# Seven products of quarters in the feed-forward of an AdaLN block, with factors summed by accumulating transfers

## The chip, the cores and the metric

One Trainium2 chip; the kernel runs on 1 of its cores. The metric is the device time of one execution in microseconds (us), smaller is better. Engines: PE multiplies matrices, DVE (VectorE), ACT (ScalarE) and POOL (GpSimd) do elementwise work, SP issues transfers; each engine works through its own queue of instructions in order. DVE and ACT read PE's results from PSUM banks; POOL works on SBUF only. Transfers (DMA) are issued from SP's, ACT's or POOL's queue.

## The reference

All data are float32: x is [4, 1024, 512], c [4, 512], eight factors of [512, 512].

```python
mod = (_silu(c) @ wmod).reshape(4, 6, 1, -1)
sa, ca, ga, sb, cb, gb = (mod[:, 0], mod[:, 1], mod[:, 2], mod[:, 3], mod[:, 4], mod[:, 5])
ga = (2 * (ga >= 0) - 1) * jnp.maximum(jnp.abs(ga), 0.25)       # gb likewise
h = _layernorm(x) * (1 + ca) + sa
# attention: q = h @ Wq.T and k = h @ Wk.T have 64 columns, shared by all 16 heads
x = x + ga * (merge(softmax(q @ k.T) @ split(h @ Wv.T)) @ Wo.T)
h = _layernorm(x) * (1 + cb) + sb
x = x + gb * (einsum('btd,rde->bte', h, factors) / sqrt(8) + bias)
```

Since the scores are the same for all heads, the value and output weights multiply into one 512x512 matrix (`wvo`), and since the feed-forward is a sum over the eight factors, they add into one 512x512 matrix (`fsum`).

## The kernel before

A batch is 1024 tokens: 8 tiles of 128 tokens (`NT`), two groups of 4 tiles (`GT`). All of the order is written by hand: a `Plan` collects calls with a beat (a number), sorts them by beat and emits them so; calls with the same beat keep the order in which they were entered. `pe(n, ...)` puts PE work at the present beat and moves it on by n beats; `at(beat, ...)` puts other work beside it. Each engine then runs its instructions in the order of emission, waiting by semaphores that the framework derives from the tiles.

Per batch there are these stages:

- `project`: q and k of each group (L393 to L421). Then `plan_scores_and_y`: eight rounds of a y tile (h times the scaled `wvo`, four matmuls of 512 columns, L483) and a tile of scores (L430). For each score tile DVE finds the maximum (L443) and ACT the exponents (L444); each pair of tiles is then transposed by DVE in 32x32 blocks (`turn_probs`, L450) and rearranged by 16 SP transfers of 64 KB (`move_probs`, L325 to L335). `sum_y` makes sums of quarters of y, on DVE for batch 0 and on POOL for the others (L488 to L499).
- `plan_f` of the batch before: `f_tile` (L542) multiplies each tile of h by the scaled factor sum `fb`, four matmuls of 512 columns into one PSUM bank, and DVE adds the bank to x (L549). A finished tile is stored and, where there is a batch after next, a tile of x is loaded in its place, both by POOL's queue.
- `plan_o`: probabilities times y, for pairs of tiles, in seven products of quarters instead of eight (Strassen's way, in Winograd's form). `sum_probs` (L464) makes sums of quarters of the probabilities on DVE. The seven products of a pair (L517 to L538) accumulate in three PSUM banks (y, q, x); after each product DVE adds the bank to the quarter of x where it belongs (L534), while the bank keeps its contents for the next product. A later product into the same bank therefore waits for this addition.

Layer norms are planned beside the attention products: `plan_ln1` for the next batch's first norm, `plan_ln2` for this batch's second. Both take statistics on DVE (L293), the power on POOL (`rstd`, L300), normalise (L309; ACT needs `center`'s product first, DVE does not), transpose on DVE (`turn_h`), move by 16 SP transfers (`move_h`) and apply scale and shift on ACT (`shift_h`, L354). `add_bias` (L555) adds the gated bias to x on POOL.

The last batch has no scores to hide behind: there the plan runs the feed-forward's first group of batch 2, the attention products of batch 3, then the second group of batch 2 and both groups of batch 3 (L709 to L722).

At the start (`plan_start`, L566) the weights, x and the six blocks of `wmod` are loaded, `wvo` is multiplied (L174) and copied out by ACT (L180), the modulation rows are made (L193 to L246), the first layer norm is transposed on PE (L380, `first_out` L389) and the factors are loaded in halves by POOL's queue and added by POOL (`load_factor`, `add_factor`, L251 to L269). Tiles share buffers by tag: "s" has two buffers (sums of probabilities), "yt" and "qT"/"kT" one, PSUM has two banks "y", two double banks "sc", and one each of "q" and "x".

## Time and profile before

| what | time |
|---|---|
| median of 3 runs | 536.98 us (536.24 to 539.12) |
| the profiled execution | 538.23 us |
| its span in the profile | 536.4 us |
| first attention product of batch 0 starts | 88.37 us |
| attention products of batch 1, 2, 3 start | 216.6, 336.7, 443.1 us |
| attention products of batch 3 end | 491.4 us |
| matmuls of `f_tile` (256 records) | 110.5 us busy, 0.592 us mean |
| DVE additions of `f_tile` (32) | 0.685 us mean |
| POOL additions of factors (14) | 2.39 us mean, 33.4 us |
| mean granted PE clock | 0.986 |

A record's duration on PE includes the pipeline; the pace of PE is read from the start of one stage to the start of the next. Durations of DVE, ACT and POOL are those of one instruction from start to end, and the next instruction can start a little before the end. The profile puts an engine's idle time down to what released it. A matmul of this program appears as two records.

### The profile page before, as it was taken

What the parts mean: (1) busy time and instruction counts of PE and PEld (TensorE: products, weight loads), DVE (VectorE), ACT (ScalarE), POOL (GpSimd) and SP (SyncE); (2) the same over time, 40 slices, a digit from 0 to 9 for tenths busy, and PEclk for the clock granted to TensorE, in tenths of its full rate; (3) what the DMA queues carried; (4) which work ended last, traced back from release to release, by engine and by line L of the source; (5) the groups of instructions that cost most, each with busy time, mean ns of one, the idle gap of its engine ahead of it and who ended that gap; (6) DMA issues with size and microseconds to landing.
All of it is one profiled execution on the core that took longest, in us unless ns stands there. A gap on an engine that the chain in (4) does not pass through costs nothing.

```text
span 536.4 us, 5575 instructions
## 1 busy us (share of the span) xinstructions
PE 520.4 (97%) x1738; PEld 306.6 (57%) x1738; DVE 347.6 (65%) x568; ACT 131.5 (25%) x206; POOL 198.0 (37%) x170
## 2 busy tenths in 40 slices
PE   8988998799999999999999999999999999999997
PEld 4343334688743344888743344888743348887442
DVE  3448699899765546689665545789665673784611
ACT  1133322212255410222155310232155310001020
POOL 1038487563144162243145072244144060450600
PEclk9997999799999999999999999999999999999999
DMA  9993589864537679523536679423536677005352
GB/s 321 381 388 116 146 156 216 139 132 106 77 51 106 93 138 227 166 69 79 78 50 104 98 148 226 155 64 80 78 50 110 96 130 139 6 5 76 102 134 78
DMA packets 223342, 68.60 MB, mean 128 GB/s; under 512 B 206528, under 2 KB 207040, under 8 KB 223312
## 3 DMA queue, kind: packets, MB, share of 16 engines
q1 hardware_dynamic: 216704, 48.30, 46.9%
q0 software_dynamic: 5504, 18.88, 10.9%
q10 hardware_dynamic: 1104, 1.06, 0.6%
q8 instruction: 14, 0.23, 0.2%
q14 instruction: 16, 0.13, 0.1%
HBM read 28.33 MB, written 8.41 MB: 68 GB/s over the span
## 4 chain that ended last, share of the span: by engine, by line
PE 88%; DVE 4%; SPq 2%; DMA 2%; ACT 2%; issue 1%; ACTq 0%; DVEq 0%
PE ps_o_y L526 21%; PE ps_f L545 20%; PE ps_y L483 17%; PE ps_o_q L526 10%; PE ps_sc L430 6%; PE ps_o_x L526 5%; PE ps_qk L403 5%; PE ps_wvo L174 3%; SPq L335 2%; PE ps_mod L193 1%; DMA wos<-in_woT_dram 1%; DMA pt<-pr 1%; DVE s L472 1%; DVE pr L453 1%; ACT hT L387 1%
## 5 line engine op out<-in xcount | busy, mean ns | idle before, releaser
L483 PE MATMUL ps_y<-w,hT 128*128 128x512 f32 x256 | 119.2, 609 | 0.0
L545 PE MATMUL ps_f<-f,hT 128*128 128x512 f32 x256 | 110.5, 592 | 0.0
L483 PEld LDWEIGHTS ps_y<-w,hT 128*128 128x128 f32 x256 | 46.8, 192 | 69.2 <-issue 67.6
L545 PEld LDWEIGHTS ps_f<-f,hT 128*128 128x128 f32 x256 | 48.6, 190 | 60.8 <-issue 59.6
L300 POOL TENSOR_TENSOR r<-v,mhalf 128x4 f32<-128x4 f32 x16 | 18.0, 1126 | 148.0 <-DVE v L298 130.9
L354 ACT ACTIVATE hT<-hT,chan,chan 128x512 f32<-128x512 f32 x56 | 41.0, 805 | 116.1 <-DMA hT<-st 116.1
L526 PE MATMUL ps_o_y<-y,pt 128*128 128x256 f32 x256 | 58.5, 379 | 0.0
L549 DVE TENSOR_TENSOR x<-ps_f,x 128x512 f32<-128x512 f32 x32 | 21.9, 685 | 50.7 <-PE ps_f L545 50.7
L526 PEld LDWEIGHTS ps_o_y<-y,pt 128*128 128x128 f32 x256 | 48.6, 190 | 8.3 <-issue 1.9
L293 DVE BATCH_NORM_STATS2 bn<-x 128x6 f32<-128x512 f32 x64 | 43.3, 677 | 6.7 <-DMA x<-in_x_dram 6.7
L555 POOL TENSOR_TENSOR x<-x,bc_gbias 128x512 f32<-128x512 f32 x32 | 43.9, 1394 | 6.1 <-DVE st L319 5.4
L317 ACT ACTIVATE st<-x,m,r 128x512 f32<-128x512 f32 x24 | 17.6, 803 | 112.1 <-DVE m L305 72.5
L443 DVE TENSOR_REDUCE nm<-ps_sc 128x1 f32<-128x1024 f32 x32 | 38.3, 1206 | 5.6 <-PE ps_sc L430 5.6
L534 DVE SCALAR_TENSOR_TENSOR x<-ps_o_y,ri,x 128x256 f32<-128x256 f32 x64 | 30.2, 471 | 17.6 <-PE ps_o_y L526 17.4
L281 POOL TENSOR_TENSOR f<-fsum,bc_gb 128x512 f32<-128x512 f32 x16 | 20.7, 1324 | 54.7 <-DMA bc_gb<-rows_gb 54.7
L444 ACT ACTIVATE pr<-ps_sc,nm 128x1024 f32<-128x1024 f32 x32 | 35.7, 1117 | 19.9 <-DVE nm L443 15.6
L339 DVE STREAM_TRANSPOSE st<-st 128x512 f32<-128x512 f32 x56 | 37.0, 689 | 5.5 <-ACT st L317 5.2
L430 PE MATMUL ps_sc<-kT,qT 64*128 64x512 f32 x128 | 38.8, 663 | 0.0
L453 DVE STREAM_TRANSPOSE pr<-pr 128x2048 f32<-128x2048 f32 x16 | 36.9, 2306 | 2.6 <-DMA pt<-pr 1.7
L269 POOL TENSOR_TENSOR fsum<-fsum,factors 128x1024 f32<-128x1024 f32 x14 | 33.4, 2388 | 11.7 <-DMA factors<-in_factors_dram 11.6
L526 PE MATMUL ps_o_y<-yt,s 128*128 128x256 f32 x128 | 32.1, 396 | 5.0 <-DVE x L534 5.0
L451 DVE RECIPROCAL ri<-den 128x2 f32<-128x2 f32 x16 | 2.6, 165 | 52.5 <-ACT pr L444 52.5
(81 smaller groups left out, 633.2 us busy)
## 6 DMA issues: line engine op xcount, KB each, us to landing
pt<-pr SPq DMA_DIRECT2D x256, 64.0 KB, 2.3
hT<-st SPq DMA_DIRECT2D x224, 64.0 KB, 2.2
factors<-in_factors_dram POOLq DMA_DIRECT2D x14, 512.0 KB, 5.1
wm<-in_wmod_dram SPq DMA_DIRECT2D x6, 1024.0 KB, 9.7
out_dram<-x POOLq DMA_DIRECT2D x24, 256.0 KB, 3.5
x<-in_x_dram SPq DMA_DIRECT2D x16, 256.0 KB, 8.9
x<-in_x_dram POOLq DMA_DIRECT2D x16, 256.0 KB, 4.6
out_dram<-x SPq DMA_DIRECT2D x8, 256.0 KB, 2.0
```

The lines of the kernel that those rows point to most:

```text
L269: nc.gpsimd.tensor_tensor(fsum[:, k, :], fsum[:, k, :], fac[n], ALU.add)
L293: nc.vector.bn_stats(s, xt[b, t])
L339: nc.vector.transpose(s, s)
L354: eng.activation(v, v, AF.Identity, bias=shift, scale=scale)
L430: nc.tensor.matmul(ps_sc[b, i][:, ts(h, 512)], qT[h * R : (h + 1) * R, ts(i, P)], kT[h * R : (h + 1) * R, :], start=True, stop=True,)
L443: nc.vector.tensor_reduce(nm, ps_sc[b, i], AX.X, ALU.max, negate=True)
L444: nc.scalar.activation(probs[b, p][:, :, k].rearrange("p c j e -> p j c e"), ps_sc[b, i].rearrange("p (j c e) -> p j c e", j=NT, c=NQ), AF ...
L453: nc.vector.transpose(v, v)
L483: nc.tensor.matmul(ps, h_rows(1, b, t, kc), wb[b][:, kc, :], start=(kc == 0), stop=(kc == KC - 1))
L526: nc.tensor.matmul(ps, a[:, ts(j, P)], bb[:, j, :], start=(tag is not None and j == 0), stop=(j == GT - 1), skip_group_check=tag is None,)
L545: nc.tensor.matmul(ps, h_rows(2, b, t, kc), fb[b][:, kc, :], start=(kc == 0), stop=(kc == KC - 1))
L555: nc.gpsimd.tensor_tensor(xt[b, t], xt[b, t], bcs["gbias", b], ALU.add)
```

## The change

Every feed-forward group but the last of batch 3 is computed in seven products of quarters: a pair of tiles (two tiles of a group, two apart), the two halves of the 512 features and the two halves of the output columns are the quarters. `product` is the former `o_product` made general; `sum_h` makes the sums of h for a group, `sum_f` those of the factors for a batch. The sums of h take a buffer "s", those of the factors the buffer that q and k of the next batch had (now one tile "qk"), in batch 3 the "yt" buffer; some sums are written over a quarter that is no longer needed. They are on DVE for batches 0 to 2 and on POOL for batch 3. In `plan_f` each product takes 2 beats.

The factors are loaded whole, 1 MB each, into `fsum`, the first by a plain transfer, the other seven by transfers that add; POOL's additions go.

The second layer norm is normalised by ACT instead of DVE for group 0 of every batch and both groups of the last; the additions of the bias are planned 8 to 72 beats later; sums of probabilities, transposes and their moves get other beats, `turn_probs` comes in four pieces, and `move_blocks` goes by columns first.

At the start x and cT are loaded from ACT's queue and the output weights from SP's, batch 0's projections use the banks "sc", the last four modulation rows a bank "y", and the copies of `wvo` come later.

```diff
--- before.py
+++ after.py
@@ -130,14 +130,13 @@
     def load_weights(cc):
         nc.sync.dma_start(out=wvs[:, cc, :], in_=wv[ts(cc, P), :])
-        nc.scalar.dma_start(out=wos[:, cc, :], in_=woT[ts(cc, P), :])
+        nc.sync.dma_start(out=wos[:, cc, :], in_=woT[ts(cc, P), :])
     for cc in range(KC - 1):
         load_weights(cc)
-        load_x(0, cc)
-        if cc == 0:
-            nc.scalar.dma_start(out=cTs, in_=cT.rearrange("(kc p) b -> p kc b", p=P))
-    load_x(0, KC - 1)
+        load_x(0, cc, nc.scalar)
+    load_x(0, KC - 1, nc.scalar)
+    nc.scalar.dma_start(out=cTs, in_=cT.rearrange("(kc p) b -> p kc b", p=P))
     load_wmod(0)
     load_wmod(1)
@@ -175,9 +174,9 @@
...
+    def wvo_out(kc):
+        nc.scalar.copy(wvo[:, kc, :], pw[kc // 2][:, ts(kc % 2, 512)])
     row_tiles = [sp.tile([B, 3, D], F32, tag="s", name=f"rows_{h}") for h in range(2)]
@@ -186,8 +185,8 @@
...
-    def mod_products(ms):
-        ps = psum_mm(f"ps_mod_{ms[0]}", "q")
+    def mod_products(ms, tag):
+        ps = psum_mm(f"ps_mod_{ms[0]}", tag)
@@ -246,27 +245,15 @@
-    def load_factor(n):
...
+    def sum_factor(r):
         if r == 0:
+            nc.gpsimd.tensor_copy(fsum[0:1, 0, 0:1], chans[1][0:1, 0, 0:1])
         nc.gpsimd.dma_start(
+            out=fsum, in_=factors[r].rearrange("(kc p) e -> p kc e", p=P),
+            accum_op=ALU.bypass if r == 0 else ALU.add,
+        )
@@ -330,8 +317,8 @@
             dst = dst.rearrange("p (r w) -> p r w", r=NQ)
-        for r in range(NQ):
-            for c in range(NQ):
+        for c in range(NQ):
+            for r in range(NQ):
@@ -394,11 +381,9 @@
         if g == 0:
-            qkT[b] = (
-                qkp.tile([2 * R, T], F32, tag="qT", name=f"qT_{b}"),
-                qkp.tile([2 * R, T // 2], F32, tag="kT", name=f"kT_{b}"),
-            )
-        ps = psum_mm(f"ps_qk_{b}_{g}")
+            qk = qkp.tile([2 * R, 3 * T // 2], F32, tag="qk", name=f"qk_{b}")
+            qkT[b] = qk[:, :T], qk[:, T:]
+        ps = psum_mm(f"ps_qk_{b}_{g}") if b else psum("sc", T, f"ps_qk_{b}_{g}")[:, :512]
@@ -447,9 +432,10 @@
-    def turn_probs(b, p):
-        nc.vector.reciprocal(rinv[b][:, 2 * p : 2 * p + 2], den[b, p])
-        v = probs[b, p].rearrange("p c k j e -> p (c k j e)")
+    def turn_probs(b, p, c):
+        if c == 0:
+            nc.vector.reciprocal(rinv[b][:, 2 * p : 2 * p + 2], den[b, p])
+        v = probs[b, p][:, c].rearrange("p k j e -> p (k j e)")
@@ -500,53 +486,113 @@
...
+    PLACE = {1: (0, 0), 5: (1, 1), 6: (0, 1), 2: (0, 0), 7: (1, 1), 3: (0, 1), 4: (1, 0)}
+    BANK = {1: "y", 6: "y", 7: "y", 4: "y", 5: "q", 3: "q", 2: "x"}
+    SUMS = {5: 0, 6: 1, 3: 2}
+    TERMS = {5: 0, 6: 1, 4: 2}
+    LEFT = {1: (0, 0), 2: (0, 1), 4: (1, 1), 7: (1, 0)}
+    RIGHT = {1: (0, 0), 2: (1, 0), 3: (1, 1), 7: (0, 1)}
+    ps_p = {}
+    def product(key, n, lefts, rights, add):
+        first = n in (1, 5, 2)
+        if first:
+            ps_p[key, BANK[n]] = psum(BANK[n], H, f"ps_{'_'.join(map(str, key))}_{BANK[n]}")
+        ps = ps_p[key, BANK[n]]
+        for j, (left, right) in enumerate(zip(lefts, rights)):
+            nc.tensor.matmul(
+                ps, left, right, start=(first and j == 0), stop=(j == len(lefts) - 1),
+                skip_group_check=not first,
+            )
+        add(ps, *PLACE[n])
+    def o_product(b, p, n):
+        a = S[b, p][:, SUMS[n]] if n in SUMS else quarter(b, p, *LEFT[n])
+        if n in TERMS:
+            y = YT[b][:, TERMS[n]]
...
+    SF, TF = {}, {}
+    KH = KC // 2
+    def f_left(b, g, ih, kh):
+        v = hT[2, b, g].rearrange("p (k t w) -> p k t w", k=KC, t=GT)
+        return v[:, ts(kh, KH), ts(ih, GT // 2), :].rearrange("p k t w -> p k (t w)")
+    def f_right(b, kh, e):
+        return fb[b][:, ts(kh, KH), ts(e, H)]
+    def sum_h(b, g, n, eng):
+        if n == 0:
...
+        u = SF[b, g]
+        a11, a12, a21, a22 = [f_left(b, g, i, k) for i in range(2) for k in range(2)]
+        o, i0, i1 = [
+            (u[:, 0], a21, a22), (u[:, 1], u[:, 0], a11), (a21, a11, a21), (u[:, 2], a12, u[:, 1])
+        ][n]
+        eng.tensor_tensor(o, i0, i1, ALU.add if n == 0 else ALU.subtract)
+    def sum_f(b, n, eng):
+        if n == 0:
+            pool, tag = (qkp, "qk") if b + 1 < B else (yp, "yt")
...
+        u = TF[b]
+        b11, b12, b21, b22 = [f_right(b, k, e) for k in range(2) for e in range(2)]
+        o, i0, i1 = [
+            (u[:, 0], b12, b11), (u[:, 1], b22, u[:, 0]),
+            (b12 if b + 1 < B else u[:, 3], b22, b12), (u[:, 2], b21, u[:, 1]),
+        ][n]
+        eng.tensor_tensor(o, i0, i1, ALU.subtract)
+    def f_product(b, g, m, n):
+        a = SF[b, g][:, SUMS[n]] if n in SUMS else f_left(b, g, *LEFT[n])
+        f = TF[b][:, TERMS[n]] if n in TERMS else f_right(b, *RIGHT[n])
+        if n == 7 and b + 1 == B:
+            f = TF[b][:, 3]
+        def add(ps, k, e):
+            xi = xt[b, f_pair(g, m)[k]][:, ts(e, H)]
+            nc.vector.tensor_tensor(xi, ps, xi, ALU.add)
+        product(
+            ("f", b, g, m), n,
+            [a[:, k, ts(m, P)] for k in range(KH)], [f[:, k, :] for k in range(KH)], add,
+        )
+    def f_pair(g, m):
+        return g * GT + m, g * GT + GT // 2 + m
@@ -560,8 +606,9 @@
         if k:
-            at(plan.now + 7, turn_probs, b, p)
-            at(plan.now + 8, move_probs, b, p)
+            for c in range(NQ):
+                at(plan.now + 7 + 1.6 * c if p + 1 < NP else plan.now + 12 + 3 * c, turn_probs, b, p, c)
+            at(plan.now + (12 if p + 1 < NP else 22), move_probs, b, p)
     def plan_start():
@@ -574,10 +621,12 @@
             pe(8, wvo_chunk, cc)
-        pe(8, mod_products, [0, 1])
+        pe(8, mod_products, [0, 1], "q")
         at(plan.now, mod_row, 1, nc.vector)
         at(plan.now, mod_row, 0, nc.scalar)
         pe(4, wvo_chunk, KC - 1, range(2))
+        at(plan.now, wvo_out, 0)
+        at(plan.now, wvo_out, 1)
         for m, plus in ((1, 1.0), (0, 0.0)):
@@ -585,16 +634,16 @@
             at(plan.now, first_out, 0, kc)
-        for n in range(2 * NR):
-            at(plan.now + 10 * max(0, n - 3), load_factor, n)
-            if n >= 2:
-                at(plan.now + 10 * max(0, n - 1), add_factor, n)
+        at(plan.now, wvo_out, 2)
+        at(plan.now, wvo_out, 3)
+        for r in range(NR):
+            at(plan.now + 24 * r, sum_factor, r)
         pe(8, project, 0, 0)
         at(plan.now, qk_out, 0, 0)
         for kc in range(KC):
             pe(1, turn_first, 1, kc)
             at(plan.now, first_out, 1, kc)
...
@@ -653,15 +702,17 @@
...
+        eng = nc.scalar if g == 0 or b + 1 == B else nc.vector
+        at(ready + 4, center, 2, b, g)
         for j in range(GT):
-            at(ready + 5 + 2 * j, normalize, 2, b, g, j, nc.vector)
+            at(ready + 4 + 2 * j, normalize, 2, b, g, j, eng)
         for c in range(NQ):
             at(ready + 13 + 2 * c, turn_h, 2, b, g, c)
         at(ready + 19.5, move_h, 2, b, g)
         for j in range(GT):
-            at(ready + 16, add_bias, b, g * GT + j)
-        for kc in range(KC):
-            at(ready + 55, shift_h, 2, b, g, kc, nc.scalar)
+            at(ready + (24 if b + 1 == B else 76 if g == 0 else 36) + 4 * j, add_bias, b, g * GT + j)
+        for kc in range(KC):
+            at(ready + (48 if b + 1 == B else 55), shift_h, 2, b, g, kc, nc.scalar)
@@ -673,8 +724,8 @@
-            at(s - (44 if b else 16) + 2 * n, sum_probs, b, 0, n)
-            at(s - (30 if b else 0) + 2 * n, sum_probs, b, 1, n)
+            at(s - (26 if b else 16) + 3 * n, sum_probs, b, 0, n)
+            at(s + 2 + 4 * n if b else s + 2 * n, sum_probs, b, 1, n)
@@ -692,34 +743,70 @@
+    def plan_f(b, groups):
+        pairs = [(g, m) for g in groups for m in range(GT // 2)]
+        queue = nc.gpsimd if b + 1 < B else nc.sync
+        def done(t):
...
+        def fourth(g, m):
+            pe(2, f_product, b, g, m, 4)
+            done(f_pair(g, m)[1])
+        for i, (g, m) in enumerate(pairs):
+            end = i + 1 == len(pairs)
+            for n in (1, 5, 4, 6, 2, 3, 7) if not end else (1, 5, 4, 6, 2, 7, 3):
+                if n != 4:
+                    pe(2, f_product, b, g, m, n)
+                    if n == 3:
+                        done(f_pair(g, m)[0])
+                elif i:
+                    fourth(*pairs[i - 1])
+        fourth(*pairs[-1])
+    def plan_sums_h(b, g, beat, eng=nc.vector):
+        for n in range(4):
+            at(beat + 3 * n, sum_h, b, g, n, eng)
+    def plan_sums_f(b, beat, eng=nc.vector):
+        for n in range(4):
+            at(beat + 2 * n, sum_f, b, n, eng)
     for b in range(B):
         last = b + 1 == B
         if b > 0:
-            plan_f(b - 1, range(GT if last else NT))
+            plan_f(b - 1, range(1 if last else 2))
         plan_o(b)
         plan_scale_f(b, plan.now + (30 if not last else -60))
         if not last:
+            s = plan.now
             for g in range(2):
                 pe(8, project, b + 1, g)
                 at(plan.now, qk_out, b + 1, g)
             plan_scores_and_y(b + 1)
+            plan_sums_h(b, 0, s + 56)
+            if b + 2 < B:
+                plan_sums_h(b, 1, s + 76)
+            plan_sums_f(b, plan.now - 7)
         else:
-            plan_f(b - 1, range(GT, NT))
-            plan_f(b, range(NT))
+            plan_sums_h(b - 1, 1, plan.now - 20)
+            plan_sums_f(b, plan.now + 2, nc.gpsimd)
+            plan_sums_h(b, 0, plan.now + 12, nc.gpsimd)
+            plan_f(b - 1, range(1, 2))
+            plan_f(b, range(1))
+            for t in range(GT, NT):
+                pe(8, f_tile, b, t)
+                at(plan.now + 2, store, b, t, nc.sync)
```

## The prediction

> **What bounds the kernel now.** I read the page first: how busy each engine is, and the chain that ended last.
>
> ```profile
> span 536.4 us, 5575 instructions
> ...
> PE 520.4 (97%) x1738; PEld 306.6 (57%) x1738; DVE 347.6 (65%) x568; ACT 131.5 (25%) x206; POOL 198.0 (37%) x170
> ...
> PEclk9997999799999999999999999999999999999999
> ...
> PE 88%; DVE 4%; SPq 2%; DMA 2%; ACT 2%; issue 1%; ACTq 0%; DVEq 0%
> ```
>
> PE sets the end. Its clock is below full only in slices 4 and 8 (40 to 54 us and 94 to 107 us). So I read the chain in order of time for what PE's stages cost, then the list of PE's waits (us in total, times, longest) for where it stands still.
>
> ```profile
> 189.12 27.47 PE ps_f L545 x64
> 216.58 1.73 PE ps_o_y L526 x8
> ...
> 491.43 41.21 PE ps_f L545 x96
> ```
>
> ```profile
> PE ps_o_y L526 <- DVE x L534: 5.0, 1, 5.0
> ...
> PE ps_qk L403 <- ACT hT L387: 0.9, 1, 0.9
> PE ps_mod L193 <- ACT hT L387: 0.9, 1, 0.9
> PE ps_hT L380 <- ACT kT L421: 0.7, 1, 0.7
> ```
>
> A feed-forward tile is 27.47/8 = 3.434 us (eight PE records, 0.429 us each); an attention product of eight 256-wide records is 1.727 us, 0.216 us each. One beat of the plan is 3.43/8 = 0.43 us. After 101.4 us PE runs without a gap; all waits lie before. The long one (92.6 to 97.66 us) is put down to a DVE addition, so I read DVE's order of time there, and at the last batch's first feed-forward group, with POOL beside it.
>
> ```profile
> 80.97 2.58 DVE L499 TENSOR_TENSOR y<-y 128x256 f32<-128x256 f32 x1
> ...
> 84.90 2.83 DVE L472 TENSOR_TENSOR s<-pt 128x512 f32<-128x512 f32 x1 [0.19 <-DMA pt<-pr]
> ...
> 88.78 2.08 DVE L499 TENSOR_TENSOR yt<-y,yt 128x256 f32<-128x256 f32 x1
> 90.79 0.41 DVE L499 TENSOR_TENSOR y<-y 128x256 f32<-128x256 f32 x1
> ```
>
> ```profile
> 84.84 2.33 POOL L269 TENSOR_TENSOR fsum<-fsum,factors 128x1024 f32<-128x1024 f32 x1 [0.55 <-DMA factors<-in_factors_dram]
> ```
>
> ```profile
> 435.38 2.93 DVE L472 TENSOR_TENSOR s<-s,pt 128x512 f32<-128x512 f32 x1
> 438.23 0.68 DVE L472 TENSOR_TENSOR pt<-pt 128x512 f32<-128x512 f32 x1
> ```
>
> ```profile
> 435.38 2.36 POOL L499 TENSOR_TENSOR yt<-y,yt 128x1024 f32<-128x1024 f32 x1
> ```
>
> The same 256-wide DVE subtraction takes 0.41 us alone and 2.08 to 2.58 us beside a POOL addition; a 512-wide one 0.68 alone, up to 2.93. A DVE operation on two SBUF tensors stands still while POOL adds two SBUF tensors. This price decides two places below, with opposite signs.
>
> **Part 1, the products.** Seven of eight groups (14 pairs of tiles) go from 2 x 3.434 = 6.867 us to seven products of two 256-wide matmuls, four records each: 7 x 4 x 0.216 = 6.04 us. PE saves 0.82 us a pair, 14 x 0.82 = **11.5 us**, on the path. (512 columns as two halves cost 0.432 against 0.429 us; that is in it.) The skill's page Perfetto Trace Analysis, section Matmuls, speaks against smaller matmuls in general; the rows put that at 0.6%. By the rule without the rows the saving could not be sized; by the rows it is 11.5.
>
> What this adds to DVE: seven PSUM additions of 256 columns a pair for two of 512. No row has this operation; its bounds are the attention's 256-wide scalar_tensor_tensor (0.47 us, next one starting 0.39 later) above and half the 0.69 us feed-forward addition below. I take 0.39: 28 additions in a two-group stage are 10.9 us. With four transposes (2.4), four sums (2.4) and four statistics (3.3) that is 19 us of the stage's 24.2, 79%. A bank's next product comes two products (1.73 us) after the one before ended, so an addition may start about 1.2 us late before PE waits. Where DVE's single operations are 0.6 to 0.8 us, as in batches 0 and 1, they fit: 0 taken. If DVE falls behind there, rival A is the price.
>
> **Part 2, the sums.** Each four-quarter set is four 512-wide tensor_tensor, 0.6 us apart: 2.4 us. Six token sets and three factor sets run on DVE (22 us), 20 normalisations of 0.87 us leave it for ACT (25% busy). In the scores' stage they lie under PE, where scores have two banks and 8 beats of y between them; moved bias additions (8 x 1.39 us on POOL) can stand in their way there, for at most 1.4 us each, and nothing on PE waits for that before the stage's end. The factor sums start 7 beats (3 us) before the products, after the last reduce, and end about as product 1 starts; product 5 needs only the first. 0 taken.
>
> **Part 3, the last batch's first group.** Here the stage has only 28 beats, so the sums of probabilities (planned 26 beats before its end) fall at beats 2 to 11, on top of POOL's three y sums (430.1 to 437.7 us in the trace). Before, a tile's bank had 3.4 us and PE did not notice. I walked DVE's queue by hand: the first sum waits for POOL until 3.3 us after the stage's start, the second until 6.4, the last until 11.5; behind them stand the additions of products 6, 3 and 1, for which PE's products 7, 5 and 6 of the next pair wait. Product 6 of the second pair starts near 12.5 instead of 7.8 us: **+4.5** (bounds 0, if the two interleave luckily, and +7, all three blocked for 2.36).
>
> **Part 4, the end.** The seven products bring the last group's tiles forward from 27.5 to 24.2 us after the attention's end. Its layer norm must follow: before, the shift began at 517.28, 25.9 us after. Its statistics had to queue behind an addition that waits 3.4 us for a tile; now 0.9: -2.6 us. Normalising on ACT (4 x 0.8) takes DVE's place (3.9 with its stalls), and no bias addition stands beside it. The 16 SP transfers (0.63 us each, 10 us) and landing (2.3) then end near 21 us: just in time. The transposes wait at DVE's head for ACT until about 7.8 us and hold two additions: **+1.5** for PE (0 to +4, the upper if the shift is late by what it was before). POOL's eight sums of the last batch (8 x 1.3 us after the 1.0 us power) end near 16 us; product 3 needs the last at 16.4: 0, but close.
>
> **Part 5, the start.** Projections move to the scores' banks, so the q bank isn't waited for (0.7 us), the four modulation rows take a y bank (0.9), and two wvo copies go behind the first hT pieces (about 0.4): PE's project of group 1 ends near 42.1 instead of 44.0. The gate's rows no longer meet POOL's addition (2.45 us at 42.27, 0.41 later for the same form), so they end before it: the gate's broadcast starts at 42.1 instead of 45.49, **-3.4** (bounds -1.5, if only the bank waits count, and -3.6). The loads' queues are only exchanged; weights still come before PE's first product at 6.4, and the cT load, which lands by 3.9 now, isn't needed before 18.5.
>
> **Part 6, the factors.** Fourteen POOL additions (33.4 us) go. DVE's blocked time from 78 to 91 us goes with them: 0.84 + 2.17 + 2.15 + 1.67 = 6.8 us, against 0.9 for transposes in four pieces. PE's 5.04 us wait and the slow products behind it (3.78 and 1.94 for 1.73 each) are 7.3 us; I take **-6** (0 if the probabilities' transfers then come late, -7.3 all). The price is eight serial accumulating transfers of 1 MB. No row has one. Bounds: below, the same bytes at the 390 GB/s of 30 to 40 us, twice for reading and writing, 5.4 us; above, twice the 9.7 us that the 1 MB wmod loads take, 19.4. I take 8 to 13, nearer the plain loads. The first lands near 41; the eighth is issued at 41 + 6T, and POOL's scaling of the next weights stands behind it, needed by the y stage at about 142 in the new time: free up to T = 16.6 us. As for issuing, the trace has 0.73 us for each factor load, beside a DVE that is busy 80% and more. The skill (SBUF — State Buffer, section SBUF: two separate sides) warns that such a POOL issue can take 3.1 instead of 0.62 us while DVE holds the shared port. By that page the eight would cost 20 us more of POOL's time, in the chain of transfers, and the sum is unchanged while T stays under about 14; no issue in this trace shows it.
>
> **Sum.** -11.5 + 4.5 + 1.5 - 3.4 - 6 = -14.9. The profiled span 536.4 becomes 521.5; the median of the runs, 536.98, is 0.6 above that span, which gives **522**.
>
> **Rivals.** A: DVE falls behind in every product stage. For it: 79% load in one queue, with additions behind sums and transposes; against it: single operations under 0.8 us and 1.2 us of slack. Two stages of four pairs at the 2.3 us a pair of part 3: +18, less a third since POOL's sums are missing there, +12: 534. B (slower): the accumulating transfer is at its upper bound, POOL's queue holds the weights' scaling, and y of batch 1 waits. It decides from T = 16.6; at T = 20 the scaling starts at 162 instead of 142: +20, 542. For it: read, add and write on engines that are 60 to 90% busy then; against: 512 KB loads land in 3.7 to 5.2 us there. C: the transfers of probabilities give way to the accumulation, the start's part 6 yields nothing and parts 3 and 4 stand at their upper ends: 522 + 6 + 2.5 = 531.
>
> **Numbers.** Forecast 0.70, A 0.08, B 0.10, C 0.12. The forecast's own ends: all gains full and no stalls, 515; stalls at 7 and 4 with half the start, 529. With C the range is 515 to 532. Half a per cent (2.7 us) is what a measurement of this kernel tells from no change. Faster by more: forecast, C and half of A, 0.86; within: 0.04; slower: B, 0.10.
>
> **What would show it.** PE's line for the products at 0.216 us a record; the seven-product stages 24.2 us long in batches 0 and 1, 12.1 plus some 4.5 in the last batch's first group, with DVE's sums of probabilities at 2 us and more there; PE's 5.0 us wait gone and o of batch 0 starting near 85; accumulating loads landing in 8 to 13 us. The prediction is wrong if the products' stages show PE waiting for DVE throughout, or POOL waiting for a factor past 140 us.

## The result, and the profile after

The changed kernel is slower: 573.64 us (median of 4 runs, 572.1 to 574.25) against 536.61 us for the kernel before beside it (4 runs, 535.73 to 539.12). The ratio is 1.068, 95% interval 1.064 to 1.072. The profiled execution has a span of 572.5 us, against 536.4.

The page of the changed kernel, its totals, its slices of the granted TensorE clock, and the engines' shares of the chain that ended last:

```profile
span 572.5 us, 6130 instructions
...
PE 521.1 (91%) x1906; PEld 342.5 (60%) x1906; DVE 385.1 (67%) x710; ACT 146.0 (26%) x226; POOL 173.5 (30%) x153
...
PEclk9997998978899979999999979999999989999999
...
PE 36%; DVE 21%; issue 10%; SPq 8%; DMA 6%; POOL 4%; ACT 3%; DVEq 0%; ACTq 0%; POOLq 0%
```

PE held 88% of the chain before and holds 36% now. Its busy time hardly changed (520.4 to 521.1 us): what the products save is spent again, most of it at a low clock (below). The rest of the span, in which it stands still, grew from 16.0 to 51.4 us. PE's list of waits (us in total, times, longest) says for what:

```profile
PE ps_f_y L509 <- DVE x L576: 16.6, 7, 5.3
PE ps_o_q L509 <- DVE x L526: 9.3, 1, 9.3
PE ps_o_y L509 <- DVE x L526: 7.5, 2, 5.0
PE ps_f_q L509 <- DVE tf L566: 5.8, 2, 2.9
PE ps_sc L415 <- ACT qk L406: 4.9, 4, 1.3
```

Four of the five name a DVE instruction, but that is only the last link; what DVE waited for is different in each stage. So the next reading is by stage, from the start of one of PE's stages to the start of the next in PE's order of time (us; "forecast" is what the parts of the prediction give for that row):

| stretch | before | after | difference | forecast |
|---|---|---|---|---|
| start until attention product of batch 0 | 88.4 | 83.2 | -5.2 | with the next row: -9.4 |
| attention, batch 0 | 56.3 | 71.7 | +15.4 | |
| attention, batches 1, 2, 3 | 48.4 each | 48.4 each | 0 | 0 |
| q, k, scores and y of batches 1, 2, 3 | 44.3 each | 46.4 to 46.5 | +6.5 in sum | 0 |
| feed-forward of batches 0 and 1 | 27.5, 27.5 | 34.2, 34.3 | +13.5 in sum | -6.6 |
| first feed-forward group of batch 2 | 13.7 | 20.7 | +6.9 | +2.9 |
| the rest, from the end of batch 3's attention | 45.1 | 44.1 | -1.0 | -1.8 |

The differences add up to the 36.1 us between the spans.

**The border to the feed-forward.** DVE's order of time at the start of batch 0's feed-forward, then POOL's:

```profile
201.51 1.22 DVE L428 TENSOR_REDUCE nm<-ps_sc 128x1 f32<-128x1024 f32 x1
202.65 2.45 DVE L566 TENSOR_TENSOR tf<-f 128x512 f32<-128x512 f32 x1
205.20 2.65 DVE L566 TENSOR_TENSOR tf<-f,tf 128x512 f32<-128x512 f32 x1
207.78 0.68 DVE L566 TENSOR_TENSOR f<-f 128x512 f32<-128x512 f32 x1
...
208.98 0.41 DVE L576 TENSOR_TENSOR x<-ps_f_y,x 128x256 f32<-128x256 f32 x1
```

```profile
202.21 2.34 POOL L485 TENSOR_TENSOR yt<-y,yt 128x1024 f32<-128x1024 f32 x1 [9.03 <-ACT y L472]
204.51 2.79 POOL L485 TENSOR_TENSOR y<-y 128x1024 f32<-128x1024 f32 x1
```

A sum of factors takes 0.68 us when alone (fourth line) and 2.45 and 2.65 us beside POOL's sums of y. Both begin for the same reason: the last tile of scores and y is out, so DVE's last maximum and ACT's last copy of y end within about half a microsecond of each other. The first product's addition (L576) stands behind all four sums and starts at 208.98 us, 7.7 us after the stage did; PE waits 2.93 us for the first sum and 3.10 for that addition. The Trainium skill (SBUF — State Buffer, section Who interferes with whom) says that a DVE instruction with two SBUF inputs contends with a GpSimd instruction that reads SBUF; these rows, 0.68 against 2.45 and 2.65 us, agree.

**A wait costs more than its length.** The granted clock around that wait, in stretches of 2 us (us; busy us of PE, PE's weight loads, DVE, ACT, POOL with their counts; clock; DMA share; GB/s):

```profile
206.00:208.00 2.00, 0.35 (x2) 0.00 (x0) 2.00 (x2) 0.00 (x0) 1.30 (x1) 0.65 0.50 75
208.00:210.00 2.00, 0.56 (x1) 0.50 (x2) 2.00 (x6) 0.00 (x0) 0.00 (x0) 0.50 0.46 68
210.00:212.00 2.00, 2.00 (x6) 1.61 (x5) 0.82 (x2) 0.00 (x0) 0.00 (x0) 0.50 0.65 98
212.00:214.00 2.00, 2.00 (x7) 1.59 (x7) 0.74 (x2) 0.00 (x0) 0.00 (x0) 0.64 0.62 92
214.00:216.00 2.00, 2.00 (x11) 1.77 (x10) 1.65 (x4) 0.00 (x0) 0.95 (x2) 1.00 0.45 67
```

PE is fully busy again from 210 us, but at half clock until past 213: 6 and 7 records in 2 us, then 11. Summed in stretches of 1 us, PE stands still in this stage for 7.3 us and loses another 2.0 (busy time times one minus clock); 34.2 less both is 24.9, the forecast 24.2 and little more. The three seven-product stages before the end lose 5.8 us this way, the attention of batch 0 another 5.8 (2.0 before). The prediction priced waits, and of the clock only what followed the one wait that went.

**Attention of batch 0.** SP's order of time before (x = number of transfers):

```profile
72.45 38.54 SPq L335 DMA_DIRECT2D pt<-pr  x48
```

After, SP again, then a few lines of DVE, PE and ACT:

```profile
65.67 35.95 SPq L322 DMA_DIRECT2D pt<-pr  x32
...
102.94 22.05 SPq L322 DMA_DIRECT2D pt<-pr  x16
125.10 32.21 SPq L322 DMA_DIRECT2D hT<-st  x48
```

```profile
127.06 0.69 DVE L458 TENSOR_TENSOR s<-pt 128x512 f32<-128x512 f32 x1 [12.04 <-DMA hT<-st]
```

```profile
128.20 3.62 PE L509 MATMUL ps_o_q<-y,s 128*128 128x256 f32 x8 [9.29 <-DVE x L526]
143.71 3.78 PE L509 MATMUL ps_o_y<-yt,s 128*128 128x256 f32 x8 [4.99 <-DVE x L526]
```

```profile
136.80 2.93 ACT L341 ACTIVATE hT<-hT,chan,chan 128x512 f32<-128x512 f32 x4 [24.70 <-DMA hT<-st]
139.63 2.91 ACT L304 ACTIVATE st<-x,m,r 128x512 f32<-128x512 f32 x4
```

Before, 48 of these moves of probabilities were out between 72.45 and 111.0 us; now they begin at 65.67 and the last 16 end at 125.0, though DVE had turned the last pair of tiles by 93.15. DVE's sum of the last pair of probabilities starts at 127.06 (the trace puts the wait down to a move of hT; the instruction reads `pt`, whose last move is issued by 125.0), and PE waits 9.29 us for an addition queued behind it. The second wait is a queue on ACT: the normalisation (L304) stands behind scale and shift of another group (L341), which waits for a slow move of hT; DVE's transposes wait for the normalisation, and additions for the transposes.

### The profile page after: what moved, and what is told of

It reads as the page before. It is cut to its first block, busy times and chain, and to the rows that moved or that the text cites. A ratio compares the mean times of both kernels' runs of the same rounds, so it can differ in the third digit from the quotient of the medians.

```text
span 572.5 us, 6130 instructions
## 1 busy us (share of the span) xinstructions
PE 521.1 (91%) x1906; PEld 342.5 (60%) x1906; DVE 385.1 (67%) x710; ACT 146.0 (26%) x226; POOL 173.5 (30%) x153
## 4 chain that ended last, share of the span: by engine, by line
PE 36%; DVE 21%; issue 10%; SPq 8%; DMA 6%; POOL 4%; ACT 3%; DVEq 0%; ACTq 0%; POOLq 0%
PE ps_o_y L509 11%; SPq L322 8%; PE ps_o_q L509 5%; PE ps_y L469 5%; PE ps_f_y L509 5%; DMA pt<-pr 3%; PE ps_o_x L509 3%; DVE pr L439 3%; DVE sf L554 3%; DVE tf L566 2%; PE ps_f L588 2%; DVE st L306 2%; PE ps_sc L415 2%; DVE nm L428 2%; PE ps_f_q L509 2%
## 5 line engine op out<-in xcount | busy, mean ns | idle before, releaser
L304 ACT ACTIVATE st<-x,m,r 128x512 f32<-128x512 f32 x44 | 32.2, 802 | 188.9 <-DVE m L292 162.2
L341 ACT ACTIVATE hT<-hT,chan,chan 128x512 f32<-128x512 f32 x56 | 40.9, 803 | 58.8 <-DMA hT<-st 57.1
L326 DVE STREAM_TRANSPOSE st<-st 128x512 f32<-128x512 f32 x56 | 37.2, 689 | 18.4 <-ACT st L304 18.3
L415 PE MATMUL ps_sc<-qk 64*128 64x512 f32 x128 | 39.6, 654 | 5.5 <-ACT qk L406 4.9
L439 DVE STREAM_TRANSPOSE pr<-pr 128x512 f32<-128x512 f32 x64 | 42.8, 690 | 1.5 <-DMA hT<-st 0.6
L509 PE MATMUL ps_o_q<-y,s 128*128 128x256 f32 x128 | 32.0, 395 | 9.3 <-DVE x L526 9.3
L509 PEld LDWEIGHTS ps_o_q<-y,s 128*128 128x128 f32 x128 | 25.3, 199 | 13.4 <-DVE x L526 9.7
L576 DVE TENSOR_TENSOR x<-ps_f_y,x 128x256 f32<-128x256 f32 x56 | 23.1, 417 | 14.3 <-PE ps_f_y L509 14.1
L509 PEld LDWEIGHTS ps_o_y<-yt,s 128*128 128x128 f32 x128 | 25.5, 201 | 12.0 <-DVE x L526 8.3
L472 ACT COPY y<-ps_y 128x512 f32<-128x512 f32 x32 | 18.7, 585 | 52.4 <-PE ps_y L469 52.4
```

Source lines behind the costliest of these rows:

```text
L304: eng.activation(dst, src, AF.Identity, bias=rm[ln, b, g][:, j : j + 1], scale=r)
L326: nc.vector.transpose(s, s)
L341: eng.activation(v, v, AF.Identity, bias=shift, scale=scale)
L415: nc.tensor.matmul(ps_sc[b, i][:, ts(h, 512)], qT[h * R : (h + 1) * R, ts(i, P)], kT[h * R : (h + 1) * R, :], start=True, stop=True,)
L439: nc.vector.transpose(v, v)
L509: nc.tensor.matmul(ps, left, right, start=(first and j == 0), stop=(j == len(lefts) - 1), skip_group_check=not first,)
```

## The experiments

Times are of one execution, v2's the median of four; the readings by stage are of the profiled execution. The kernel before ran beside them at 538.65 us (e1, e2, e3, e5), 535.97 (e4, e7, e8, v1) and 536.26 (e6, e9, v1s, v2: the median of seven, 533.13 to 538.35). Executions of one kernel thus differ by up to 5 us. Part of this lies in the start: batch 0's attention begins between 79.6 and 83.2 us in the six kernels (after, e1, e3, e6, e7, e8) whose start is the same. So a few us between two totals show nothing by themselves, and each experiment is read by its stages (us):

| kernel | time | attention, batch 0 | scores' stages | feed-forward 0, 1, 2 (one group) |
|---|---|---|---|---|
| before | 536.6 | 56.3 | 44.3, 44.3, 44.3 | 27.5, 27.5, 13.7 |
| after | 573.6 | 71.7 | 46.5, 46.4, 46.5 | 34.2, 34.3, 20.7 |
| e1, whole products | 555.3 | 69.2 | 49.8, 46.4, 46.5 | 27.5, 27.5, 13.7 |
| e2, plain transfers | 563.2 | 63.3 | 46.5, 46.5, 50.8 | 33.6, 34.1, 16.7 |
| e3, sums on POOL | 563.8 | 73.3 | 46.4, 46.4, 49.8 | 28.6, 29.0, 18.5 |
| e4, POOL adds factors | 554.8 | 57.3 | 49.8, 46.5, 49.8 | 29.0, 34.0, 16.5 |
| e5, moves as before | 573.5 | 72.4 | 46.5, 46.4, 50.5 | 33.6, 34.2, 18.0 |
| e6, DVE normalises | 568.6 | 67.6 | 50.3, 46.4, 46.5 | 32.3, 34.1, 20.9 |
| e7, e3 and statistics by arrival | 560.9 | 73.5 | 49.8, 49.8, 46.5 | 24.7, 24.5, 19.9 |
| e8, bias as before | 559.0 | 68.9 | 44.7, 45.0, 44.7 | 32.9, 33.2, 16.5 |
| e9, e4 and e8 together | 552.8 | 59.3 | 44.7, 45.2, 45.0 | 33.3, 33.1, 16.7 |
| v1, all at once | 534.6 | 61.7 | 45.8, 46.0, 45.8 | 24.3, 24.2, 13.1 |
| v1s, v1 and a later shift | 525.4 | 59.5 | 44.8, 45.1, 44.9 | 24.4, 24.2, 13.1 |
| v2, v1s and POOL adds factors | 525.8 | 57.5 | 44.8, 45.1, 44.8 | 24.3, 24.2, 13.1 |

**e1: the products undone.** Every feed-forward group goes back to whole tiles; the rest of the change stays.

```diff
-        pairs = [(g, m) for g in groups for m in range(GT // 2)]
...
-                    pe(2, f_product, b, g, m, n)
+        for t in [g * GT + j for g in groups for j in range(GT)]:
+            pe(8, f_tile, b, t)
...
-            plan_sums_h(b, 0, s + 56)
...
-            plan_sums_f(b, plan.now - 7)
```

> The changed kernel with the feed-forward in whole tiles again (four 512-wide matmuls) and no sums for it; everything else as changed. Theory 1 (the sums and additions on DVE, blocked by POOL, make PE wait in the product stages and cost 20 us, the start's accumulating transfers another 10): the three feed-forward stages between the attention stages go back to 27.5, 27.5 and 13.7 us, the first attention stage still ends near 155 us, total near 553 us. Rival (the loss is in the start, the norms and the transfers, the products themselves gain as forecast): the stages fall only to 27.5 while the loss stays elsewhere, total near 585 us.

Measured 555.27 us: 18.4 less than after. The feed-forward stages are those of before to 0.1 us. So the products with their sums, as planned, cost 18 us where they were forecast to save 5.5 (11.5 less the 6.0 of parts 3 and 4), and another 18.7 us come from the rest of the change.

**e2 and e4: the accumulation.** e2 leaves out the sum of the factors (only the last factor remains in `fsum`); the eight transfers keep their bytes and their order.

```diff
-            accum_op=ALU.bypass if r == 0 else ALU.add,
+            accum_op=ALU.bypass,
```

> The changed kernel with all eight factor transfers plain, none adding (the feed-forward then uses the last factor alone, the sum of the factors is left out). Theory 1 (adding doubles the time of the transfer engines, the probabilities' moves of batch 0 come late and PE waits 9.3 us): a factor lands in 5 to 6 us instead of 9.4, the move of the last pair ends near 112 instead of 125 us, the first attention stage ends near 143 instead of 155, total near 562 us. Rival 1 (the move of the last pair was planned too late): lands earlier, but the 9.3 us wait stays above 6, total 570 or more.

e4 takes `load_factor` and `add_factor` of before, with their beats, into the changed kernel:

```diff
-        for r in range(NR):
-            at(plan.now + 24 * r, sum_factor, r)
+        for n in range(2 * NR):
+            at(plan.now + 10 * max(0, n - 3), load_factor, n)
+            if n >= 2:
+                at(plan.now + 10 * max(0, n - 1), add_factor, n)
```

> The changed kernel with the factors loaded in halves and added by POOL as before. Theory 1 (the accumulating transfers cost the 15 us of batch 0's attention stage by delaying the probabilities' moves, and save the POOL additions that held DVE up): the probabilities' last moves are issued by 114 us instead of 125, the 9.3 us wait goes, a wait of about 5 us near 92 us comes back; q and k of batch 1 start at 145 to 149 instead of 154.8; total 564 to 568. Rival (the attention stage is late because of the new order of the second norm on ACT, whatever loads the factors): q and k of batch 1 at 153 or later, total 572 or more.

e2: 563.24 us; e4: 554.78, below its expectation of 564 to 568. Batch 0's attention falls from 71.7 to 63.3 and to 57.3 us. SP's order of time in e4, then in v1s (below), where no factor is under way beside the first 32 moves:

```profile
68.62 24.16 SPq L335 DMA_DIRECT2D pt<-pr  x32
...
94.10 13.36 SPq L335 DMA_DIRECT2D pt<-pr  x16
```

```profile
70.85 21.95 SPq L322 DMA_DIRECT2D pt<-pr  x32
...
94.12 12.71 SPq L322 DMA_DIRECT2D pt<-pr  x16
```

32 moves take 21.95 us with no factor beside them, 24.16 in e4, 30.52 beside the plain 1 MB transfers of e2, 35.95 beside the accumulating ones. The last factor transfer is issued at 94.64 us in e4, at 104.73 in e2 and at 114.31 in the changed kernel, so the last 16 moves meet fewer of them too. A 1 MB factor lands after 9.4 us (median) when it accumulates and 7.0 when it does not. In the stretch from 80 to 130 us of the changed kernel, SP's queue holds 49% of the DMA engines' time and the factors' queue 47%. So the way the factors are loaded is worth 14.3 of the 15.4 us: moves of probabilities that PE is waiting for share the DMA engines with transfers that nobody needs before 180 us. e4's gain beyond that stage is in the feed-forward, 5.2 us in batch 0 and 4.1 in batch 2 (e9 shows why it is not the same each time); two of its scores' stages are 3.3 us longer, at a clock of 0.92.

**e5: the transposes and moves of probabilities at their beats of before.**

```diff
-                at(plan.now + 7 + 1.6 * c if p + 1 < NP else plan.now + 12 + 3 * c, turn_probs, b, p, c)
-            at(plan.now + (12 if p + 1 < NP else 22), move_probs, b, p)
+                at(plan.now + 7 + 1.6 * c, turn_probs, b, p, c)
+            at(plan.now + 12, move_probs, b, p)
```

> The changed kernel with the last pair's four transposes and its move at the same beats as the other pairs' (7 to 12 beats after its scores instead of 12 to 22). Rival 1 (planned too late): the 9.3 us wait of PE in batch 0 falls under 3 us and the first attention stage ends near 147 us, total near 566. Theory 1 (adding transfers): SP's queue is full until 102 us anyway, the wait stays 7 us or more, total within 2 us of 573; in the later product stages DVE gets its transposes a little earlier, no more than 2 us either way.

573.52 us, no change: the order in which the moves are planned is not what delays them.

**e6: the second norm's first group normalised by DVE again** (batches 0 to 2).

```diff
-        eng = nc.scalar if g == 0 or b + 1 == B else nc.vector
+        eng = nc.scalar if b + 1 == B else nc.vector
```

> The changed kernel with the first group of the second norm normalised by DVE again in batches 0 to 2 (the last batch stays on ACT). Theory 1 (in batch 0 the normalisation stands in ACT's queue behind a scale and shift that waits for a slow move, and DVE's transposes and the products' additions behind it): the 5.0 us wait near 144 us goes, q and k of batch 1 start at 149 to 152 instead of 154.8, other stages as they were, total 568 to 571. Rival (the wait only moves to the next thing that waits for SP's moves): 573 or more.

568.64 us; the wait at 144 us is gone, and q and k of batch 1 start at 147.2 instead of 154.8. The stage itself is 4.1 us shorter; the rest of the 7.6 is an earlier start of the stage (79.6 instead of 83.2), which varies between kernels that leave the start alone (82.2 in e8, 80.1 in e7). The two waits in front of it are 5.0 and 8.5 us here, 2.6 and 9.3 in the changed kernel.

**e8: the bias additions at their beat of before.**

```diff
-            at(ready + (24 if b + 1 == B else 76 if g == 0 else 36) + 4 * j, add_bias, b, g * GT + j)
+            at(ready + (24 + 4 * j if b + 1 == B else 16), add_bias, b, g * GT + j)
```

> The changed kernel with the bias additions of batches 0 to 2 back at their beat of before (16 beats after ready). Theory 1 (the new beats of the bias additions let an idle POOL run them just where DVE wants the center and normalises at the start of the next scores' stage, 2.1 us in each of three stages): scores' stages from the first q and k to the first feed-forward product 44.3 to 45 us instead of 46.5, total 567 to 569. Rival (the 2.1 us come from the projections' longer queue on ACT, which now also normalises): stages stay at 46.5, total 572 to 574.

558.95 us: the scores' stages came back as theory 1 says (44.7 to 45.0), but the total fell by 14.7 where 5 to 7 were expected. First the part expected. In the changed kernel, DVE's center and normalisation at the start of the scores' stage, and POOL beside it:

```profile
158.55 1.22 DVE L292 SCALAR_TENSOR_TENSOR m<-mv,r 128x4 f32<-128x4 f32 x1 [1.21 <-POOL r L287]
159.69 2.02 DVE L306 TENSOR_SCALAR st<-x,mv,r 128x512 f32<-128x512 f32 x2
161.63 0.67 DVE L404 COPY qk<-ps_qk 64x512 f32<-64x512 f32 x1
```

```profile
158.49 2.49 POOL L601 TENSOR_TENSOR x<-x,bc_gbias 128x512 f32<-128x512 f32 x2
```

DVE in e8:

```profile
154.82 0.16 DVE L292 SCALAR_TENSOR_TENSOR m<-mv,r 128x4 f32<-128x4 f32 x1 [1.20 <-POOL r L287]
155.20 1.00 DVE L306 TENSOR_SCALAR st<-x,mv,r 128x512 f32<-128x512 f32 x2 [0.21 <-issue]
```

POOL had nothing else to do, so the first group's additions, planned 60 beats and more later in the order, ran as soon as POOL reached them, directly behind the power, on top of DVE; the copy of q and k, and PE behind it (1.34 us), are late. In e8 center and the first two normalisations take 0.16 and 1.00 us instead of 1.22 and 2.02, and the three stages are 5.1 us shorter in sum. The part not expected: in batch 2's feed-forward group DVE comes to the factor sums early enough that all four are over (449.14 us) just as POOL's sum of y starts (449.11), so that collision does not happen, and the stage is 4.2 us shorter. DVE's last factor sum there, then POOL's sum of y:

```profile
448.45 0.69 DVE L566 TENSOR_TENSOR tf<-f,tf 128x512 f32<-128x512 f32 x1
```

```profile
449.11 2.36 POOL L485 TENSOR_TENSOR yt<-y,yt 128x1024 f32<-128x1024 f32 x1 [15.35 <-ACT y L472]
```

The rest of the 14.7 lies in the attention of batch 0 (2.7 us), the other two feed-forward stages (1.3 and 1.1) and the start (1.0); what caused it is not shown.

**e9: e4 and e8 together** (both diffs).

> The changed kernel with both reversed: factors loaded in halves and added by POOL, and the bias additions of batches 0 to 2 at their beat of before. Alone they gave back 18.9 and 14.7 us. Theory 1 (separate causes, in batch 0's attention stage and in the scores' and feed-forward stages): together 31 to 33.6 us, 540 to 543 us. Rival (they share one cause, a DVE that is late everywhere): clearly less than the sum, 546 to 552.

552.83 us: 20.8 us back, not the 33.6 of the two alone, so my theory of separate causes missed. The scores' stages are repaired, batch 0's attention nearly so. What remains is the border to the feed-forward; DVE's order of time there, then POOL's:

```profile
188.62 0.68 DVE L579 TENSOR_TENSOR tf<-f 128x512 f32<-128x512 f32 x1
189.40 0.69 DVE L579 TENSOR_TENSOR tf<-f,tf 128x512 f32<-128x512 f32 x1
190.01 2.83 DVE L579 TENSOR_TENSOR f<-f 128x512 f32<-128x512 f32 x1
192.76 2.82 DVE L579 TENSOR_TENSOR tf<-f,tf 128x512 f32<-128x512 f32 x1
```

```profile
189.52 2.78 POOL L498 TENSOR_TENSOR yt<-y,yt 128x1024 f32<-128x1024 f32 x1 [13.88 <-ACT y L485]
192.26 2.78 POOL L498 TENSOR_TENSOR y<-y 128x1024 f32<-128x1024 f32 x1
```

Two of the four sums are blocked, PE waits 5.42 us. How many are hit depends on a microsecond in DVE's arrival: none in e8's batch 2, one of them in e4's batch 0, two here. That makes batch 0's feed-forward 4.3 us longer than in e4; another 3.6 us lie before the first attention product (84.6 us against 81.0), where the two kernels are the same. So single effects do not add up.

**e3: all sums of h and of factors on POOL.**

```diff
-            plan_sums_h(b, 0, s + 56)
+            plan_sums_h(b, 0, s + 56, nc.gpsimd)
...
-            plan_sums_f(b, plan.now - 7)
+            plan_sums_f(b, plan.now - 7, nc.gpsimd)
```

> The changed kernel with the sums for batches 0 to 2 that ran on DVE in the scores' stage (sums of h and of factors) on POOL instead, at the same beats. Theory 1 (DVE late by its two-tensor sums and blocked by POOL at the border of the stage): the DVE operations of 2.5 to 2.8 us there vanish, PE's waits in the first two product stages fall from 10 to under 3 us each, total near 558 us. Rival 2 (DVE is simply overloaded by additions): the waits stay within 30%, total above 568. If POOL becomes the late one, PE waits for POOL's sums instead, at the first 'q' product.

563.82 us, between the 558 of its theory and the 568 of its rival, with feed-forward stages of 28.6 and 29.0 us: on one engine the sums queue and do not collide, and no wait is left at the border. What is left lies later; DVE and PE:

```profile
218.83 0.69 DVE L280 BATCH_NORM_STATS2 bn<-x 128x6 f32<-128x512 f32 x1 [2.67 <-DMA x<-in_x_dram]
```

```profile
221.03 1.13 PE L509 MATMUL ps_f_q<-tf,sf 128*128 128x256 f32 x4 [1.96 <-DVE x L576]
```

A pair of tiles is finished together and late, so x of the batch after next is loaded late, and DVE's statistics for it hold up the additions behind them. **e7** keeps e3 and takes the statistics in the order of arrival (tiles 0, 2, 1, 3), all of them a few beats later, and the power behind them 2 beats later:

```diff
-        for j in range(GT):
-            at(first + 8 * j, stats, 1, b, g * GT + j)
+        if b > 1 and g == 0:
+            for j, beat in ((0, -22), (2, -10), (1, -3), (3, 4)):
+                at(first + 24 + beat, stats, 1, b, j)
```

> Built on the run with all sums on POOL (563.8 us, feed-forward stages 28.6, 29.0 and 18.5 us), and takes the first group's layer-norm statistics of the next batch later and in the order in which x now arrives (tiles 0, 2, 1, 3, since pairs of tiles come free together). Theory 1 (what is left over the ideal 24.2 us in those stages is DVE standing at its statistics for x that is still under way, with the products' additions behind it): f of batches 0 and 1 come to 24.5 to 26 us, no PE wait over 1 us there, total 556 to 559. Rival (DVE simply has too much to do beside seven additions a pair): the stages stay at 28 to 29 us and the total at 562 to 564.

560.87 us. The two stages are 24.7 and 24.5 us: within 0.5 us of the forecast, without a PE wait and with 28 additions a stage on DVE. The total missed its range by 2 us: two scores' stages take 49.8 us (one in e3), and the attention of batch 2 takes 49.6 instead of 48.4. Windows of e7 (columns as above), then PE's one wait in the first of these stages:

```profile
160.40:203.40 43.00, 41.66 (x98) 15.47 (x97) 23.45 (x32) 19.96 (x33) 25.66 (x21) 0.92 0.53 84
203.40:228.10 24.70, 24.70 (x114) 20.97 (x113) 17.20 (x41) 1.69 (x3) 16.97 (x17) 1.00 0.87 182
```

```profile
166.44 2.93 PE L415 MATMUL ps_sc<-qk 64*128 64x512 f32 x6 [1.34 <-ACT qk L406]
```

The same 1.34 us wait stands in the changed kernel at 167.70 us. There the clock stays at 1.00 and this part of the stage takes 39.6 us; here it is halved from 167 to 174 us, and it takes 43.0. The work is the same. In both e3 and e7 batch 2's group is left at 18.5 and 19.9 us, by what part 3 of the prediction describes: in e3 the four sums of probabilities take 2.08, 1.83, 1.57 and 2.10 us beside POOL's sums of y, and PE waits 3.8 us in four pieces behind them.

**v1, v1s, v2: all of it mended.** v1 has e3 and e7, the second norm on ACT throughout, the bias additions at other beats (45 and 14 after the norm is ready instead of 76 and 36), four accumulating transfers before and four after batch 0's moves of probabilities, the last batch's first sums of probabilities 18 beats earlier, and a few sums and scalings at other beats. v1s also plans one scale and shift 12 beats later (74 where v1 has 62) and the sums of h for group 0 4 beats later; v2 takes e4's factors into v1s. The core of the new parts, as v1s has them:

```diff
-            at(plan.now + 24 * r, sum_factor, r)
+            if r < 4:
+                at(plan.now + (0, 24, 48, 58)[r], sum_factor, r)
...
+            for r, beat in ((4, 61), (5, 71), (6, 116), (7, 128)):
+                at(s + beat, sum_factor, r)
...
-            at(s - (26 if b else 16) + 3 * n, sum_probs, b, 0, n)
+            at(s - (44 if b + 1 == B else 26 if b else 16) + 3 * n, sum_probs, b, 0, n)
...
-            at(ready + (48 if b + 1 == B else 55), shift_h, 2, b, g, kc, nc.scalar)
+            at(ready + (48 if b + 1 == B else 74 if g == 0 else 55), shift_h, 2, b, g, kc, nc.scalar)
```

> Everything at once: statistics in the order of arrival, sums of h and of the factors on POOL, all second norms on ACT, bias additions at beats where DVE does not need its two SBUF reads, four accumulating transfers before the probabilities' moves and four behind them, the last batch's sums of probabilities 18 beats earlier. If the mechanisms named so far are the whole of the loss, the seven-product stages are 24.2 to 26, 24.2 to 26 and 12 to 14 us, batch 0's attention stage 56 to 60, scores' stages 44.3, total 512 to 522 (before: 538). If the accumulating transfers slow whatever runs beside them, batch 0 stays at 60 to 66 and the total is 522 to 532.

> The all-at-once version with the later scale and shift alone; the accumulating transfers stay. The difference to v2 is then the accumulating transfers by themselves. Expected 530 to 533: 0.9 to 1.4 us less in each of three scores' stages; in batch 0's attention stage the 11.1 us wait stays, since it hangs on the first norm's shift behind the slow moves.

> The all-at-once version (534.6 us in its look) with the factors loaded in halves and added by POOL again instead of the accumulating transfers, and with the scale and shift of the second norm's first group 12 beats later, so that ACT copies q and k first. If the accumulating transfers are what costs batch 0's attention stage its last 5 us and its 3 us later start, that stage starts at 81 us and takes 57 to 58 us instead of 61.8, the scores' stages lose 0.9 to 1.4 us each, and the total is 520 to 526 (before: 537). If they are not, 530 to 534.

v1: 534.59 us, above both of its ranges and level with the kernel before beside it (535.97, one execution each). The feed-forward stages came as expected; the scores' stages took 45.8 to 46.0 us instead of 44.3, and one 11.07 us wait in batch 0's attention was left, of the same queue on ACT that e6 shows. v1s: 525.44 us, better than its 530 to 533; I expected that wait to stay, and it became 3.91 and 2.16 us. The sixth transfer is issued at 121.9 us in v1s and at 118.2 in v1, nearer the moves of hT that ACT waits for; with one execution of each this is a reading, not shown. And 3.9 of the 9.1 us between v1 and v1s lie before the first attention product, where the two kernels are the same: PE loses 3.2 us there to a low clock in v1 and none in v1s. v2: 525.79 us (4 runs, 524.2 to 528.19) against 536.26, ratio 0.981, interval 0.976 to 0.986: 1.9% below the kernel before. That is in its range, but not by the reason that was given with it, the accumulating transfers: v1s keeps them, and its time lies among v2's four. So no cost of an accumulating transfer is seen in the total once it does not run beside the moves; batch 0's attention is 1.9 us longer in v1s. v2's page:

```profile
span 522.4 us, 6191 instructions
...
PE 507.9 (97%) x1906; PEld 336.1 (64%) x1906; DVE 343.1 (66%) x666; ACT 154.1 (30%) x238; POOL 245.7 (47%) x210
...
PEclk9998998999999999999999999999999999999999
```

PE's busy time is 507.9 us against 520.4 before: 12.5 less, about the 11.5 that the products were to save. POOL works 245.7 us instead of 173.5, and PE is still busy for 97% of the span.

## Why the prediction was wrong

The forecast was 522 us, range 515 to 532, with 0.86 on faster; measured 573.64. The direction was wrong, and neither the range nor a rival held it. Rival C's sum was also short: parts 3 and 4 both at their upper ends add 5 us, not 2.5, which makes 533, outside the stated range. By parts:

- **Part 1, the products: right in itself.** 24.2 to 24.7 us a stage in e7, v1, v1s and v2, without waits: the saving is there and DVE's additions fit. Rival A looked at the right engine, but its cause, too many additions, is not what happened: these stages hold all the additions.
- **Part 2, the sums: the step that failed most**, with "The factor sums start 7 beats (3 us) before the products, after the last reduce, and end about as product 1 starts" and "0 taken". In batch 0 the first of them starts 1.4 us after the stage (202.65 against 201.29), in batch 2 0.1 us before it (459.20 against 459.34): the last reduce, which stands in front of them, comes that late. The rows quoted at the top of the prediction, 0.68 us alone and 2.93 beside POOL's addition, were applied to the last batch's sums of probabilities only. The same collision stands at every border, where POOL's sums of y wait for the same release as DVE's sums of factors: with what follows it, the stages are 6.7 to 6.9 us above before, some 20 us off the forecast in the first two. e3 shows it (sums on POOL, no wait at the border), and so does e8's batch 2 (sums on DVE, but over before POOL starts). A second loss, statistics that wait for x (1.26 us of PE's waits in batch 0's stage of the changed kernel, 3.6 in e3's), was not in the prediction at all: a tile at a time became two tiles together, and the step that frees x was not followed on to its next reader.
- **Part 2, the bias additions:** "nothing on PE waits for that before the stage's end". PE waits 1.34 us at the stage's beginning, through the copies of q and k; the three stages are 6.5 us above before, and e8 gives 5.1 of it back. A later place in the plan is no later time than the end of the work in front of it in the queue.
- **Part 3:** forecast +4.5 for that group on top of -1.6, measured +6.9 over before. In the changed kernel the larger wait, 5.25 us, is again the factor sums (2.84 and 2.82 us). With those out of the way, e3 has the stall of part 3 alone: 3.8 us of waits and 1.5 at a low clock against 4.5, and with the sums of probabilities moved too (v1, v2) the group takes 13.1 us. The mechanism was right, and the size, 5.3 us in e3, nearly so.
- **Part 4, the end:** -1.8 forecast, -1.0 measured; a 1.54 us PE wait at 540.01 us stands where +1.5 was put.
- **Parts 5 and 6:** the attention of batch 0 does start earlier (83.2 us, 79.6 to 83.2 in kernels with the same start; "near 85" was named), and DVE's blocked time is gone. The transfer's 8 to 13 us was right too (9.4). What failed is the use of it: the eight were priced by when the last is done, "free up to T = 16.6", and not by what their bytes take from the moves beside them. The lower end of part 6 was 0 "if the probabilities' transfers then come late"; measured, start and stage together lost 10.2 us where 9.4 were to be gained. Rival C was this mechanism, at a cost of 6 us instead of some 15; rival B did not occur. The 3.1 us that the prediction takes from the Trainium skill (SBUF — State Buffer, section SBUF: two separate sides), a figure for a transfer issued from GpSimd beside a DVE copy, did not show either: issues of factors took POOL 0.85 to 1.34 us.
- **No part** held the half clock after each new wait, 9.6 us more than before in the attention of batch 0 and the three feed-forward stages.

What is not settled: why the same 1.34 us wait halves the clock in one execution and not in another, and how the 15.4 us of batch 0's attention divide between slow moves and ACT's queue; e2, e4 and e6 give overlapping shares (8.4, 14.3 and 4.1 us).

## What to carry to other kernels

When a step is added at a stage's border, list what else is released by the same event on the engine that gets in its way (here POOL and DVE); a known price of 2 us must be asked for at every such place, not only at the first one found. A transfer that nobody needs soon is not free if one that somebody needs now runs beside it: price its bytes against that neighbour, and move it out of its way. Work that moves from one engine to another should go where its queue orders it (sums on POOL behind POOL's other sums) rather than where there seems to be time.

## What the runs showed of the hardware

A halved clock follows waits as short as 1.34 us (e7) and lasts about 3 to 7 us of busy PE time, 1.4 to 3.4 us lost for each; the same wait can also leave the clock at 1.00 (the changed kernel at 167.70 us). The Trainium skill (TensorE: Matmul & The Clock Gate, Part 1) puts an idle window of about 3.4 us before the halving and calls the window free-running; a free-running window would fit the varying outcome, but the 1.34 us wait of e7 is shorter than the page's window. No run here tests which position of the window decides. An accumulating 1 MB transfer into SBUF lands in 9.4 us where a plain one of the same bytes in the same place takes 7.0 (e2; both medians of eight beside other transfers), and its issue holds POOL's queue for 1.28 us against 0.78. A DVE normalisation, with one SBUF tensor and two scalars a partition, also takes twice its time beside a POOL addition: 2.02 us for two against 1.00 (e8).
